# An SSM scan with a gated FFN behind it: when the last matmul part of a side piece is issued

## The chip, the cores and the metric

The kernel runs on one core of one Trainium2 chip. The metric is the device time of one execution in microseconds (us). The kernel before takes 2835.29 us, the median of three runs (2834.98 to 2836.63).

## The reference, cut to what matters

The input `x` holds 2 sequences of 1024 tokens with 512 features (float32). The first layer is a selective state space model, the second a gated FFN; behind each stands a layernorm over the residual sum.

```python
# layer 0, SSM: B=2, L=1024, D=512, N=R=128
xn    = x * rsqrt(mean(x*x) + 1e-6) * norm_w
xn    = xn * sigmoid((xn @ select_proj_w.T + select_proj_b) * select_gate)
xp    = xn @ x_proj_w.T                     # delta | B | C, 128 columns each
delta = softplus(xp[..., :R] @ dt_proj_w.T + dt_proj_b)
A     = -exp(A_log)
def step(h, (dt, bt, ct, xt)):              # once per token, h is [B, D, N]
    h = exp(dt[:, :, None] * A) * h + (dt * xt)[:, :, None] * bt[:, None, :]
    y = einsum('bdn,bn->bd', h, ct)
x = layernorm(x + (y + x * D_param) @ out_proj_w.T)
# layer 0, FFN: 2048 hidden features
x = layernorm(x + (silu(x @ w_gate.T) * (x @ w_up.T)) @ w_down.T)
```

## The kernel before, in words

**Groups and slots.** The 2048 tokens are cut into 64 blocks of 32 (`S`). A block has 16 groups of work, so the main loop (L673) runs over 1024 groups `k`. A group brings one scan: 128 partitions (the state index n), 32 features and 32 tokens, 1024 elements in a row (L716). `place` (L398) turns `k` into a half block `h = k // 8` and a slot `r = k % 8`.

**What one group issues.** TensorE (PE) gets four matmuls that each use 32 of its rows: two that write `bu`, the input of this group's scan (L696), and two that write `a`, the exponents of the next group's decay (L408 in `decay_mm`). ScalarE (ACT) takes two exponentials of `a` into `a_sb` (L415, `decay_exp`). VectorE (DVE) adds the carried state to the first column of `bu` (L715) and runs the scan (L716) into `h`. GpSimd (POOL) spreads `dt` and `du` over a block diagonal for later groups (`diag`, L379 and L389). The matmuls of `y` (L432, `y_round`) follow in slots 1, 4 and 7, eight rounds for each half block (`ROUNDS`, L22). `bu` and the PSUM tile of `a` have two buffers each, `a_sb` has three.

**Side work.** All else is written as Python generators that the loop steps through: `pre` prepares the inputs of the next lot of tokens (lots of 128, 128 and then 256 tokens, L69), `post` takes `y` of 128 tokens to the first layernorm, `ffn` makes the FFN of 128 tokens, and `silu` and `normalize` are short helpers. A generator yields "P" where it wants to begin a piece of matmuls, "H" while the piece has matmuls left and "E" where work of other engines follows. A *piece* is what goes into one tile of the single PSUM bank that `misc` (L158) hands out in the loop; a *part* is what is issued between two yields. `gu` (gate and up projections, L539) has 8 parts of two matmuls, `d` (down projection, L559) 16 parts of one, `op` (output projection, L480) 8 of one, `sel`, `xp` and `ss` 4 of one, `zT`, `x1T` and `uT` 2 of two transposes, `z` 2 of one, `b` one or two of four, `t0` (L307) a single part of four.

**What sets the order.** The slots 0, 2, 3, 5 and 6 get credit for side parts: `PARTS` (L23) is (4, 0, 3, 3, 0, 3, 3, 0), 16 parts for eight groups. Credit that isn't used is kept up to 6, and one group takes at most four parts (L725 to L729). `Work.tensor` (L636) takes the next part of the piece that holds the bank; when the piece is at its end the function returns False until the bank is read out, which `give_back` (L622, at the start of a slot with credit) or `others` (L629, once per group behind the exponentials) does. So a group can end one piece or begin one, but cannot do both.

**What must be ready when.** `load` (L333) fetches the operands of the next block out of DRAM at slot 0 of every second half block. Where the next block belongs to a new lot, `work.finish` (L689) first steps the side work until that lot's `pre` is done. The last steps of `pre` write two or three results, `uT` once or twice (L291) and `t0` (L314), through one and the same SBUF tile (tag "row", a single buffer) and from there to DRAM (L296, L315).

**Queues.** Every DMA is issued by SyncE (SP) in program order: weights of the FFN (L513, five buffers), `ub` and `cd` (L337, L345), `ub_d` (L259, L296), `x1`, `zT`, outputs.

**The end.** Behind the loop stand the last eight `y` rounds, and then the side work that is left, with six PSUM banks and no credit (L753).

Of the kernel before, what the change touches and what calls it, by code (L numbers as in the profile page):

```python
# [35 lines left out]
def kernel(  # L36
# [118 lines left out]

    made = {}

    def misc(name):  # L158
        return bank_pool[0].tile([P, 512], FP, tag="m", name=name)


# [3 lines left out]
    def pre(c):  # L165

        t0, n = lots[c]
        n_j, n_s = n // P, n // S
        if c == 0:
            xT = first_xT  # L170
        else:
            xT = pre_pool.tile([P, NM, TC], FP, tag="xT", name=f"xT_{c}")
            nc.sync.dma_start(xT[:, :, 0:n], x_tr[:, :, t0 : t0 + n])
        rms = pre_pool.tile([P, TC], FP, tag="rms", name=f"rms_{c}")
        low = pre_pool.tile([P, TC], FP, tag="low", name=f"low_{c}")
        dt = pre_pool.tile([P, NM, TC], FP, tag="dt", name=f"dt_{c}", bufs=2)
        u = pre_pool.tile([P, NM, TC], FP, tag="u", name=f"u_{c}")
        c_sb = pre_pool.tile([P, TC], FP, tag="c_sb", name=f"c_sb_{c}", bufs=2)
        rms, low, c_sb = rms[:, 0:n], low[:, 0:n], c_sb[:, 0:n]
        xT, dt, u = xT[:, :, 0:n], dt[:, :, 0:n], u[:, :, 0:n]  # L180
        xn = xT
        made[c] = dt, c_sb

        def matmuls(ps, w, m, rhs):
            for k in range(NM):
                nc.tensor.matmul(  # L186
                    ps[:, 0:n], w[:, k, ts(m, P)], rhs[:, k, :],
                    start=(k == 0), stop=(k == NM - 1),
                )
                yield "H" if k + 1 < NM else "E"  # L190

        yield "E"
        yield "E"
        yield "E"

        nc.scalar.activation(u, xT, AF.Square)
        yield "E"
        for m in range(NM):
            nc.scalar.activation(xT[:, m, :], xT[:, m, :], AF.Copy, scale=col(V_NORM, m))
        yield "P"  # L200
        ps = misc(f"ss_{c}")
        for k in range(NM):
            nc.tensor.matmul(  # L203
                ps[:, 0:n], ones, u[:, k, :], start=(k == 0), stop=(k == NM - 1)
            )
            yield "H" if k + 1 < NM else "E"

        nc.scalar.activation(rms, ps[:, 0:n], AF.Ln, bias=eps_r, scale=1.0 / D)
        nc.scalar.activation(rms, rms, AF.Exp, scale=-0.5)
        yield "E"  # L210
        for a in (slice(0, 2), slice(2, 4)):
            nc.gpsimd.tensor_tensor(
                xn[:, a, :], xT[:, a, :], rms.unsqueeze(1).to_broadcast([P, 2, n]), ALU.mult
            )
            yield "E"
        yield "P"


        for m in range(NM):
            ps = misc(f"sel_{c}_{m}")  # L220
            yield from matmuls(ps, sel_w, m, xn)
            nc.scalar.activation(
                u[:, m, :], ps[:, 0:n], AF.Relu,
                bias=neg[:, 1, m : m + 1], scale=neg[:, 0, m : m + 1],
            )
            nc.scalar.activation(
                dt[:, m, :], ps[:, 0:n], AF.Abs, bias=gate_b[:, m : m + 1], scale=col(V_GATE, m)
            )
            yield "P" if m + 1 < NM else "E"
        yield from softplus(dt, u)  # L230
        nc.scalar.activation(dt, dt, AF.Exp, scale=-1.0)
        yield "E"
        for a in (slice(0, 2), slice(2, 4)):
            nc.gpsimd.tensor_tensor(xn[:, a, :], xn[:, a, :], dt[:, a, :], ALU.mult)
            yield "E"
        yield "P"

        if c == 0:
            decay()

        for g, dst in ((0, low), (2, c_sb)):
            ps = misc(f"xp_{c}_{g}")
            yield from matmuls(ps, xp_w, g, xn)
            nc.scalar.copy(dst, ps[:, 0:n])
            yield "P"

        ps = misc(f"b_{c}")
        for j in range(n_j):
            for k in range(NM):
                nc.tensor.matmul(  # L250
                    ps[:, ts(j, N)], xn[:, k, ts(j, P)], xp_w[:, k, R : R + N],
                    start=(k == 0), stop=(k == NM - 1),
                )
            yield "H" if j + 1 < n_j else "E"
        bt = pre_pool.tile([P, TC // P, N], FP, tag="bt", name=f"bt_{c}")[:, 0:n_j, :]
        nc.scalar.copy(bt, ps[:, 0:n].rearrange("p (j n) -> p j n", n=N))
        for st in range(n_s):
            rows = bt[ts(st % 4, S), st // 4, :]
            nc.sync.dma_start(  # L259
                ub_d[t0 // S + st, :, :, 1, :].rearrange("g t n -> t g n"),  # L260
                rows.unsqueeze(1).to_broadcast([S, 4, N]),
            )
        yield "P"

        for a in range(0, NM, 2):
            ps = misc(f"z_{c}_{a}")
            for m in (a, a + 1):
                nc.tensor.matmul(  # L268
                    ps[:, ts(m - a, n)], dt_w[:, ts(m, P)], low, start=True, stop=True
                )  # L270
                yield "H" if m == a else "E"
            for m in (a, a + 1):
                z = ps[:, ts(m - a, n)]
                nc.scalar.activation(u[:, m, :], z, AF.Relu, bias=col(V_DTB, m))
                nc.scalar.activation(dt[:, m, :], z, AF.Abs, bias=col(V_DTB, m))  # L275
            yield "P" if a == 0 else "E"
        yield from softplus(dt, u)
        for a in (slice(0, 2), slice(2, 4)):
            nc.gpsimd.tensor_tensor(u[:, a, :], dt[:, a, :], xn[:, a, :], ALU.mult)
            yield "E"  # L280

        for j in range(n_j):
            yield "P"
            ps = misc(f"uT_{c}_{j}")
            for m in range(NM):
                nc.tensor.transpose(ps[:, ts(m, P)], u[:, m, ts(j, P)], ident)
                if m == 1:
                    yield "H"
            yield "E"
            t = pre_pool.tile([P, D], FP, tag="row", name=f"uT_{c}_{j}")  # L290
            nc.scalar.copy(  # L291
                t.rearrange("p (g m c) -> p m g c", g=4, m=NM),
                ps.rearrange("p (m g c) -> p m g c", m=NM, g=4),
            )
            for st in range(4):
                nc.sync.dma_start(  # L296
                    ub_d[t0 // S + 4 * j + st, :, :, 0, :].rearrange("g t q -> t g q"),
                    t[ts(st, S), :].rearrange("t (g q) -> t g q", g=4),
                )
            if c == 0:  # L300
                load(0)
                diag(0, 0)
                diag(0, 1)
        yield "P"
        ps = misc(f"t0_{c}")
        for m in range(NM):
            nc.tensor.matmul(  # L307
                ps[0:n_s, ts(m, P)],
                dt[:, m, :].rearrange("p (s t) -> p s t", t=S)[:, :, 0], ident,
                start=True, stop=True,  # L310
            )
        yield "E"
        t = pre_pool.tile([P, D], FP, tag="row", name=f"t0_{c}")
        nc.scalar.copy(t[0:n_s, :], ps[0:n_s, :])  # L314
        nc.sync.dma_start(dt0_d[t0 // S : (t0 + n) // S, :], t[0:n_s, :])  # L315
# [139 lines left out]
    def post(tt):  # L455
# [5 lines left out]
        nc.gpsimd.tensor_tensor(zT, zT, dq.unsqueeze(2).to_broadcast([P, NM, P]), ALU.mult)  # L461
        yield "E"
        yield "P"
        ps = misc(f"zT_{tt}")
        for s in range(4):
            nc.tensor.transpose(ps[:, ts(s, P)], yrs[tt][:, s, :], ident)
            if s == 1:
# [6 lines left out]
        x1 = post_pool.tile([P, D], FP, tag="x1", name=f"x1_{tt}", bufs=4)  # L474
        nc.sync.dma_start(x1, xf[tt])
        yield "P"
        ps = misc(f"op_{tt}")
        for half in (slice(0, 256), slice(256, 512)):
            for k in range(NM):
                nc.tensor.matmul(  # L480
# [19 lines left out]
    def ffn(tt, row):  # L500
# [17 lines left out]
        fetch(4)  # L518
        x1T = ffn_pool.tile([P, NM, P], FP, tag="x1T", name=f"x1T_{tt}")
        yield "P"  # L520
        ps = misc(f"x1T_{tt}")
        for m in range(NM):
            nc.tensor.transpose(ps[:, ts(m, P)], row[:, ts(m, P)], ident)
            if m == 1:
# [6 lines left out]
        for f in range(0, NF, 2):  # L531
            fetch(at + 4)
            yield "P"
            ps = misc(f"gu_{tt}_{f}")
            for b in range(2):
                w = pieces[at + b].rearrange("p (a k h) -> p a k h", a=2, k=NM)
                for a in range(2):
# [13 lines left out]
        for half in range(2):  # L551
            fetch(at + 4)
            yield "P"
            ps = misc(f"d_{tt}_{half}")
            for f in range(NF):
                if f == NH:
                    fetch(at + 6)
# [47 lines left out]
    class Work:  # L605


        def __init__(self):
            self.gens, self.holder = [], None

        def add(self, gen, front=False):
            item = [gen, next(gen)]
# [23 lines left out]
        def tensor(self):  # L636

            if self.holder is not None:
                if self.holder[1] != "H":
                    return False  # L640
                self.step(self.holder)
                return True
            for item in self.gens:
                if item[1] == "P":
                    self.holder = item
                    self.step(item)
                    return True
            return False

# [23 lines left out]
    for k in range(NG):  # L673
# [49 lines left out]
            for b in ROUNDS[r]:  # L723
                y_round(h - 1, b)
        credit = min(credit + PARTS[r], 6)  # L725
        for _ in range(min(credit, 4) if PARTS[r] else 0):
            if not work.tensor():
                break
            credit -= 1  # L729

        j, r4 = divmod(k, 4)
        if r4 == 3:
# [93 lines left out]
```

## Time and profile before

| what | value |
|---|---|
| median of 3 runs | 2835.29 us |
| the profiled execution: its time, and the span from its first to its last instruction | 2828.25 us, 2826.4 us |
| first scan, last scan (start, from the span's start) | 43.2 us, 2745.2 us |
| scans (L716) | 1024, mean 2286 ns |
| PE busy, DVE busy | 2711.6 us, 2518.8 us |
| `gu` matmuls (L539), `d` matmuls (L559) | busy 535.4 us, 256.9 us |
| DMA | 258.80 MB, 28% of the 16 engines' time |
| mean granted TensorE clock | 0.990 |

The table is read in two stages. Up to 2745 us the loop issues one scan after the other, and the distance from one scan's start to the next is the length of a step. Behind it come some 80 us without scans, in which PE works off what side work is left. A matmul in float32 shows as two records.

### The profile page before, as it was taken

Reading aid. Unit: us, or ns where it says so; the run is one execution under the profiler, and the core shown is the slowest. Engines: PE = TensorE matmul, PEld = TensorE weight load, DVE = VectorE, ACT = ScalarE, POOL = GpSimd, SP = SyncE. Lnnn points to the kernel's source line nnn. Section 1 sums busy time; section 2 is a strip of 40 time slices with the busy share of each in tenths; the row PEclk is TensorE's granted clock in tenths of the full one; section 3 lists DMA queues with packets and bytes.
Section 4 is the critical chain, followed back from the end, with each engine's and each line's share of the span. In section 5 each row is a group of like instructions: output and inputs, shape, how many; then the busy total and the mean of one; then the engine's idle time right before and its main releaser. Section 6 shows DMA issues by size and latency. Waiting matters only on the chain.

```text
span 2826.4 us, 59495 instructions
## 1 busy us (share of the span) xinstructions
PE 2711.6 (96%) x23744; PEld 1491.2 (53%) x23744; DVE 2518.8 (89%) x2144; ACT 1549.2 (55%) x3105; POOL 1780.9 (63%) x2016
## 2 busy tenths in 40 slices
PE   6879999999999999999999999999999999999998
PEld 4334554555555554555544555555555555555558
DVE  3999899999999999999999999999999999999980
ACT  4546555645565455654656556555555555545442
POOL 5556665666666665775667667667576666657552
PEclk7999999999999999999999999999999999999999
DMA  2002322324213232233312333133331323333336
GB/s 75 19 28 66 88 86 70 95 67 142 79 63 124 79 122 64 83 96 103 126 43 84 106 105 104 57 99 95 113 102 48 112 81 116 102 106 96 105 105 209
DMA packets 112388, 258.80 MB, mean 92 GB/s; under 512 B 11568, under 2 KB 49456, under 8 KB 112112
## 3 DMA queue, kind: packets, MB, share of 16 engines
q1 hardware_dynamic: 112112, 254.99, 28.2%
q8 instruction: 189, 3.10, 0.5%
q14 instruction: 87, 0.71, 0.1%
HBM read 242.23 MB, written 12.71 MB: 90 GB/s over the span
## 4 chain that ended last, share of the span: by engine, by line
PE 74%; DVE 18%; issue 3%; ACT 3%; POOL 1%; DMA 1%; SPq 0%; DVEq 0%; ACTq 0%; POOLq 0%
PE bu L696 28%; PE gu L539 17%; DVE h L716 16%; PE y L432 13%; PE d L559 7%; PE a L408 3%; PE sel L186 2%; PE op L480 2%; PE xp L186 1%; ACT a_sb L415 1%; DVE bu L715 1%; DMA ub_d<-uT 1%; PE b L250 1%; PE ss L203 0%; PE z L268 0%
## 5 line engine op out<-in xcount | busy, mean ns | idle before, releaser
L716 DVE TENSOR_TENSOR_SCAN h<-a_sb,bu 128x1024 f32<-128x1024 f32 x1024 | 2340.3, 2286 | 153.5 <-PE bu L696 44.6
L415 ACT ACTIVATE a_sb<-a 128x496 f32<-128x496 f32 x2048 | 1088.9, 584 | 1125.1 <-PE a L408 1049.6
L696 PE MATMUL bu<-du,ub 32*128 32x512 f32 x4096 | 1195.0, 644 | 49.4 <-DVE h L716 25.4
L408 PE MATMUL a<-ddt,a_t 32*128 32x512 f32 x4096 | 1224.1, 645 | 2.8 <-ACT t L314 2.8
L379 POOL TENSOR_TENSOR ddt<-dt,hot 128x512 f32<-128x512 f32 x512 | 533.6, 1048 | 218.6 <-PE a L408 218.6
L539 PEld LDWEIGHTS gu<-x1T,w 128*128 128x128 f32 x4096 | 479.7, 192 | 233.7 <-issue 153.6
L389 POOL TENSOR_TENSOR du<-ub,hot 128x512 f32<-128x512 f32 x512 | 535.3, 1049 | 26.7 <-PE a L408 23.3
L539 PE MATMUL gu<-x1T,w 128*128 128x128 f32 x4096 | 535.4, 282 | 11.7 <-ACT t L314 5.5
L432 PE MATMUL y<-h,cz 128*32 128x256 f32 x9208 | 526.8, 362 | 1.6 <-DVE h L716 1.0
L696 PEld LDWEIGHTS bu<-du,ub 32*128 32x128 f32 x4096 | 335.7, 184 | 345.0 <-issue 185.2
L432 PEld LDWEIGHTS y<-h,cz 128*32 128x32 f32 x9208 | 256.3, 110 | 408.9 <-issue 274.9
L408 PEld LDWEIGHTS a<-ddt,a_t 32*128 32x128 f32 x4096 | 354.7, 184 | 22.9 <-ACT a_sb L415 13.2
L559 PE MATMUL d<-w,hid 128*128 128x256 f32 x1024 | 256.9, 393 | 1.1 <-ACT dt L275 1.1
L715 DVE TENSOR_TENSOR bu<-bu,cd 128x32 f32<-128x32 f32 x992 | 183.3, 185 | 79.8 <-PE a L408 75.7
L559 PEld LDWEIGHTS d<-w,hid 128*128 128x128 f32 x1024 | 183.5, 189 | 121.6 <-issue 92.5
L577 POOL TENSOR_SCALAR gu<-gu 128x256 f32<-128x256 f32 x128 | 108.1, 844 | 198.7 <-ACT gu L547 198.0
L585 POOL TENSOR_TENSOR hid<-gu,e 128x256 f32<-128x256 f32 x128 | 92.8, 725 | 140.1 <-ACT e L583 139.2
L447 POOL TENSOR_TENSOR yc<-yc,pick 128x512 f32<-128x512 f32 x64 | 66.6, 1040 | 179.5 <-ACT yc L446 179.5
L366 POOL TENSOR_TENSOR cd<-cd,h 128x256 f32<-128x256 f32 x124 | 106.2, 857 | 43.9 <-DVE h L716 43.9
L578 POOL TENSOR_TENSOR gu<-gu 128x256 f32<-128x256 f32 x128 | 93.3, 729 | 10.7
L547 ACT COPY gu<-gu 128x512 f32<-128x512 f32 x128 | 75.2, 588 | 32.6 <-PE gu L539 32.2
L324 POOL TENSOR_TENSOR dt<-dt,u 128x512 f32<-128x512 f32 (+1 forms) x36 | 41.2, 1148 | 67.6 <-ACT dt L321 67.6
(86 smaller groups left out, 1246.0 us busy)
## 6 DMA issues: line engine op xcount, KB each, us to landing
w<-in_wgu_s_dram SPq DMA_DIRECT2D x256, 512.0 KB, 4.1
w<-in_wd_s_dram SPq DMA_DIRECT2D x128, 512.0 KB, 3.6
cd<-dt_d SPq DMA_DIRECT2D x62, 256.0 KB, 4.1
ub<-ub_d SPq DMA_DIRECT2D x64, 128.0 KB, 2.0
ub_d<-bt SPq DMA_DIRECT2D x64, 64.0 KB, 1.8
ub_d<-uT SPq DMA_DIRECT2D x64, 64.0 KB, 1.8
zT<-in_x_q_dram SPq DMA_DIRECT2D x16, 256.0 KB, 3.9
x<-in_x_dram SPq DMA_DIRECT2D x16, 256.0 KB, 3.7
```

The lines of the kernel that those rows point to most:

```text
L366: nc.gpsimd.tensor_tensor(cd, cd, last, ALU.mult)
L379: nc.gpsimd.tensor_tensor(ddts[j][:, m, :, :], made[lot_of[st]][0][:, a + m, toks(st)].unsqueeze(1).to_broadcast([P, 16, S]), hot[:, ts(i, ...
L389: nc.gpsimd.tensor_tensor(dus[j][:, m, :, :], uv[:, a + m, :].unsqueeze(2).to_broadcast([P, 16, S]), hot.unsqueeze(1).to_broadcast([P, 16, ...
L408: nc.tensor.matmul(ps, a_t[ts(g, 32), m, :], ddts[k // 4][ts(g, 32), m % 2, :, :], start=True, stop=True,)
L415: nc.scalar.activation(a_sb[:, k % 3, ts(b, 16), 1:], ps[:, :, 1:], AF.Exp, scale=-1.0)
L432: nc.tensor.matmul(ys[st][ts(m, 32), 256 * i + 4 * q0 : 256 * i + 4 * (q0 + nq)], cz[st % 3][:, at : at + 32], hs[h][:, 64 * m + q0 : 64 * ...
L539: nc.tensor.matmul(ps[:, ts(2 * a + b, P)], w[:, a, k, :], x1T[:, k, :], start=(k == 0), stop=(k == NM - 1),)
L559: nc.tensor.matmul(ps[:, 0:HD], hid[:, f, :], w[:, f % 4, :], start=(f == 0), stop=(f == NF - 1),)
L577: nc.gpsimd.tensor_scalar_max(g, g, -80.0)
L696: nc.tensor.matmul(bu[:, ts(b, 16), :], prepared[st][ts(g, 32), 1, :], dus[k // 4][ts(g, 32), m % 2, :, :], start=True, stop=True,)
L715: nc.vector.tensor_tensor(first, first, left[:, at : at + 2, i, :], ALU.add)
L716: nc.vector.tensor_tensor_scan(hs[h][:, ts(r, 32), :].rearrange("p q t -> p (q t)"), a_sb[:, k % 3, :, :].rearrange("p q t -> p (q t)"), b ...
```

## The change

`misc` now takes the number of parts of the piece that it opens and stores it in `work.left`; `Work.tensor` counts it down. The loop that hands out parts goes on while fewer than `most = min(credit, 4)` are taken, as before, and now also while at least one and fewer than five are taken and just one part of the piece is left. What is taken is subtracted from the credit, which can so become negative. A slot without credit of its own (1, 4, 7) still takes nothing.

```diff
--- before.py
+++ after.py
@@ -155,7 +155,8 @@
 
     made = {}
 
-    def misc(name):
+    def misc(name, parts):
+        work.left = parts
         return bank_pool[0].tile([P, 512], FP, tag="m", name=name)
 
 
@@ -198,7 +199,7 @@
         for m in range(NM):
             nc.scalar.activation(xT[:, m, :], xT[:, m, :], AF.Copy, scale=col(V_NORM, m))
         yield "P"
-        ps = misc(f"ss_{c}")
+        ps = misc(f"ss_{c}", NM)
         for k in range(NM):
             nc.tensor.matmul(
                 ps[:, 0:n], ones, u[:, k, :], start=(k == 0), stop=(k == NM - 1)
@@ -217,7 +218,7 @@
 
 
         for m in range(NM):
-            ps = misc(f"sel_{c}_{m}")
+            ps = misc(f"sel_{c}_{m}", NM)
             yield from matmuls(ps, sel_w, m, xn)
             nc.scalar.activation(
                 u[:, m, :], ps[:, 0:n], AF.Relu,
@@ -239,12 +240,12 @@
             decay()
 
         for g, dst in ((0, low), (2, c_sb)):
-            ps = misc(f"xp_{c}_{g}")
+            ps = misc(f"xp_{c}_{g}", NM)
             yield from matmuls(ps, xp_w, g, xn)
             nc.scalar.copy(dst, ps[:, 0:n])
             yield "P"
 
-        ps = misc(f"b_{c}")
+        ps = misc(f"b_{c}", n_j)
         for j in range(n_j):
             for k in range(NM):
                 nc.tensor.matmul(
@@ -263,7 +264,7 @@
         yield "P"
 
         for a in range(0, NM, 2):
-            ps = misc(f"z_{c}_{a}")
+            ps = misc(f"z_{c}_{a}", 2)
             for m in (a, a + 1):
                 nc.tensor.matmul(
                     ps[:, ts(m - a, n)], dt_w[:, ts(m, P)], low, start=True, stop=True
@@ -281,7 +282,7 @@
 
         for j in range(n_j):
             yield "P"
-            ps = misc(f"uT_{c}_{j}")
+            ps = misc(f"uT_{c}_{j}", 2)
             for m in range(NM):
                 nc.tensor.transpose(ps[:, ts(m, P)], u[:, m, ts(j, P)], ident)
                 if m == 1:
@@ -302,7 +303,7 @@
                 diag(0, 0)
                 diag(0, 1)
         yield "P"
-        ps = misc(f"t0_{c}")
+        ps = misc(f"t0_{c}", 1)
         for m in range(NM):
             nc.tensor.matmul(
                 ps[0:n_s, ts(m, P)],
@@ -461,7 +462,7 @@
         nc.gpsimd.tensor_tensor(zT, zT, dq.unsqueeze(2).to_broadcast([P, NM, P]), ALU.mult)
         yield "E"
         yield "P"
-        ps = misc(f"zT_{tt}")
+        ps = misc(f"zT_{tt}", 2)
         for s in range(4):
             nc.tensor.transpose(ps[:, ts(s, P)], yrs[tt][:, s, :], ident)
             if s == 1:
@@ -474,7 +475,7 @@
         x1 = post_pool.tile([P, D], FP, tag="x1", name=f"x1_{tt}", bufs=4)
         nc.sync.dma_start(x1, xf[tt])
         yield "P"
-        ps = misc(f"op_{tt}")
+        ps = misc(f"op_{tt}", 2 * NM)
         for half in (slice(0, 256), slice(256, 512)):
             for k in range(NM):
                 nc.tensor.matmul(
@@ -518,7 +519,7 @@
         fetch(4)
         x1T = ffn_pool.tile([P, NM, P], FP, tag="x1T", name=f"x1T_{tt}")
         yield "P"
-        ps = misc(f"x1T_{tt}")
+        ps = misc(f"x1T_{tt}", 2)
         for m in range(NM):
             nc.tensor.transpose(ps[:, ts(m, P)], row[:, ts(m, P)], ident)
             if m == 1:
@@ -531,7 +532,7 @@
         for f in range(0, NF, 2):
             fetch(at + 4)
             yield "P"
-            ps = misc(f"gu_{tt}_{f}")
+            ps = misc(f"gu_{tt}_{f}", 2 * NM)
             for b in range(2):
                 w = pieces[at + b].rearrange("p (a k h) -> p a k h", a=2, k=NM)
                 for a in range(2):
@@ -551,7 +552,7 @@
         for half in range(2):
             fetch(at + 4)
             yield "P"
-            ps = misc(f"d_{tt}_{half}")
+            ps = misc(f"d_{tt}_{half}", NF)
             for f in range(NF):
                 if f == NH:
                     fetch(at + 6)
@@ -606,7 +607,8 @@
 
 
         def __init__(self):
-            self.gens, self.holder = [], None
+
+            self.gens, self.holder, self.left = [], None, 0
 
         def add(self, gen, front=False):
             item = [gen, next(gen)]
@@ -638,12 +640,14 @@
             if self.holder is not None:
                 if self.holder[1] != "H":
                     return False
+                self.left -= 1
                 self.step(self.holder)
                 return True
             for item in self.gens:
                 if item[1] == "P":
                     self.holder = item
                     self.step(item)
+                    self.left -= 1
                     return True
             return False
 
@@ -723,10 +727,11 @@
             for b in ROUNDS[r]:
                 y_round(h - 1, b)
         credit = min(credit + PARTS[r], 6)
-        for _ in range(min(credit, 4) if PARTS[r] else 0):
-            if not work.tensor():
-                break
-            credit -= 1
+        done, most = 0, min(credit, 4)
+
+        while PARTS[r] and (done < most or 0 < done < 5 and work.left == 1) and work.tensor():
+            done += 1
+        credit -= done
 
         j, r4 = divmod(k, 4)
         if r4 == 3:
```

## The prediction, made before the changed kernel ran

> **What bounds the kernel now.** I read the page's busy shares and chain first, then the start of every scan in the timeline, then the largest steps, then the end.
>
> ```profile
> PE 2711.6 (96%) x23744; PEld 1491.2 (53%) x23744; DVE 2518.8 (89%) x2144; ACT 1549.2 (55%) x3105; POOL 1780.9 (63%) x2016
> PE 74%; DVE 18%; issue 3%; ACT 3%; POOL 1%; DMA 1%; SPq 0%; DVEq 0%; ACTq 0%; POOLq 0%
> L716 DVE TENSOR_TENSOR_SCAN h<-a_sb,bu 128x1024 f32<-128x1024 f32 x1024 | 2340.3, 2286 | 153.5 <-PE bu L696 44.6
> ```
>
> PE looks like the only bound. The 1023 steps between scan starts say something else: they add up to 2702.0 us, and more than half of them last 2.48 us, which is the scan and the add on DVE back to back. 1023 x 2.483 is 2540; the 162 us above sit in some 350 steps over 2.6 us. So DVE sets most steps, and PE sets those where more work came than PE can do in one step. Here are three groups with four `gu` parts each (slots 0, 2 and 3, about 998 to 1009 us), with a `y` group between the first two:
>
> ```profile
> 998.31 2.05 PE L539 MATMUL gu<-x1T,w 128*128 128x128 f32 x16
> ...
> 1003.86 2.05 PE L539 MATMUL gu<-x1T,w 128*128 128x128 f32 x16
> 1006.92 2.05 PE L539 MATMUL gu<-x1T,w 128*128 128x128 f32 x16
> ```
> ```profile
> 1002.25 2.29 DVE L716 TENSOR_TENSOR_SCAN h<-a_sb,bu 128x1024 f32<-128x1024 f32 x1
> 1004.45 0.17 DVE L715 TENSOR_TENSOR bu<-bu,cd 128x32 f32<-128x32 f32 x1
> 1004.73 2.29 DVE L716 TENSOR_TENSOR_SCAN h<-a_sb,bu 128x1024 f32<-128x1024 f32 x1
> ...
> 1010.14 0.20 DVE L715 TENSOR_TENSOR bu<-bu,cd 128x32 f32<-128x32 f32 x1 [0.47 <-PE a L408]
> 1010.44 2.29 DVE L716 TENSOR_TENSOR_SCAN h<-a_sb,bu 128x1024 f32<-128x1024 f32 x1
> ```
>
> Full groups follow on PE at 3.05 us (1003.86 to 1006.92). The first step shown is still 2.48 us, as PE had run ahead; by the third full group the lead is gone and DVE waits 0.47 us. An average of PE can't tell this: what counts is how full groups are bunched.
>
> The largest step of all, 326.90 to 336.97 us, is no bunch:
>
> ```profile
> 326.90 2.29 DVE L716 TENSOR_TENSOR_SCAN h<-a_sb,bu 128x1024 f32<-128x1024 f32 x1
> 336.66 0.20 DVE L715 TENSOR_TENSOR bu<-bu,cd 128x32 f32<-128x32 f32 x1 [7.48 <-PE a L408]
> ```
> ```profile
> 328.75 0.58 ACT L291 COPY uT<-uT 128x512 f32<-128x512 f32 x1 [1.20 <-DMA ub_d<-uT]
> 332.68 0.57 ACT L314 COPY t<-t 8x512 f32<-8x512 f32 x1 [3.33 <-DMA ub_d<-uT]
> ```
>
> Before group 112 `work.finish` forces the rest of `pre` for the third lot. In the order of PE's instructions its two `uT` stand at groups 109 and 110 and `t0` directly ahead of group 112: three copies through the one "row" buffer, each waiting for the DMAs of the one before, and the matmuls of group 112 queued behind.
>
> **The change part by part.** I counted, in the PE order of both programs, the parts that each slot with credit takes in groups 0 to 1022. Beside them is the mean step that follows such a group, from the scan starts of before: no part 41 to 43 groups (2.480 us); one 57 to 9 (2.553); two 95 to 154 (2.619); three 141 to 145 (2.554); four 306 to 284 (2.824); five 0 to 5 (no row). The total rises only from 1896 to 1913 parts, since credit limits it: a last part taken early is paid back by the next group, which gets two instead of four.
>
> *The end of the loop.* Of the 17 parts, 16 are one half of a `d` piece that leaves the end; the last part of a `gu` piece goes too, but that lay under a wait for POOL. The end of before:
>
> ```profile
> 2747.55 3.64 PE L432 MATMUL y<-h,cz 128*32 128x256 f32 x58 [1.05 <-DVE h L716]
> ...
> 2755.88 5.41 PE L480 MATMUL op<-out_w,zT 128*128 128x256 f32 x16 [1.39 <-DVE zT L471]
> 2761.12 13.98 PE L559 MATMUL d<-w,hid 128*128 128x256 f32 x64
> 2774.93 0.60 PE L523 MATMUL x1T<-ident,x 128*128 128x128 f32 x4
> 2777.59 28.85 PE L539 MATMUL gu<-x1T,w 128*128 128x128 f32 x256 [2.05 <-ACT x1T L527]
> ```
>
> From the end of `y` (2751.2) to the first `gu` (2777.6) are 26.4 us. A `d` matmul is 13.98/32 = 0.437, a part of `gu` 2 x 28.85/128 = 0.451. The changed order puts the one remaining `d` half right behind `y`, then `zT`, `op`, `x1T`. So: `d` 7.0 (it now covers the read-out of `y`), `zT` 0.6, the wait for DVE 1.4, `op` 3.5 at 0.437 each or 5.4 as here, then what `d` used to cover, the normalizing of `x1` (end of `op` 2761.3 to the end of ACT's L496 at 2764.7: 3.4), then `x1T` to `gu` 2.7. That is 18.6 to 20.5, a gain of 5.9 to 7.8. I take 7.0.
>
> *The forced stop.* The changed order has `uT` of that lot at groups 104 and 106 and `t0` at 107, five groups ahead of the due one; nothing is forced. The step of 10.07 becomes an ordinary `y` step (mean 2.544): 7.5 gained. Both `uT` and `t0` still pass the one buffer. The six later lots do that unforced; only two lost time near it, 2.3 us (step behind group 310) and 1.5 (behind 440), so the price to expect is 3.8/6 = 0.6. I take 6.9 gained, bounds 5.2 (a loss of 2.3 here too) and 7.5.
>
> *The other steps.* By the counts above, without the forced step: 2 x 2.480 - 48 x 2.553 + 59 x 2.619 + 4 x 2.554 - 22 x 2.824 + 5 x (2.824 to 3.275, a four-part step and one part more) = -0.9 to +1.4. But a two-part step can't by itself cost more than one with three parts; its row carries the bunches ahead of it. So I count bunches: steps by how many of the last three slots with credit took at least four parts (groups 32 to 1021, excess over 2.483 in before): none 0.071, one 0.111, two 0.222, three 0.239. These go from 147, 397, 297 and 148 steps to 217, 322, 344 and 106: 70 x 0.071 - 75 x 0.111 + 47 x 0.222 - 42 x 0.239 = -2.9. I take this, as it follows what the timeline shows. Bounds: if PE set every step, 17 x 0.44 = 7.4 more, and 5 x 0.45 for the five-part groups: +9.7. If PE ran dry in each of the 48 one-part groups and that hole is now filled, -48 x 0.45 + 7.4 = -14.2.
>
> DMAs and copies are the same in number. SP's weight loads move with their pieces by a few groups; SP waits for PE to free `w` buffers 858 us in all, so its queue follows PE and isn't ahead of it. I cost this at nothing; the cover is that a piece begins with its weights fetched a piece ahead.
>
> Sum: -7.0 - 6.9 - 2.9 = -16.8 us. The profiled span of 2826.4 becomes 2809.6. That execution took 2828.25, 7.0 below the median of the runs, so I carry the difference over: 2835.3 - 16.8 = 2818.5.
>
> *The clock.* Behind the forced stop the granted clock is 0.50 for 3.4 us:
>
> ```profile
> 333.40:336.80 3.40, 3.40 (x13) 1.67 (x14) 0.14 (x1) 0.25 (x1) 0.00 (x0) 0.50 0.32 89
> ```
>
> The Trainium skill ("TensorE: Matmul & The Clock Gate", section "What's actually happening") says that PE falls to half its clock after an idle window of about 3.4 us and needs a busy one to come back. The trace agrees at this place. By that rule the newly exposed 3.4 us between `op` and `x1T` would start `gu` at half rate and take 3.4/2 = 1.7 back: a sum of -15.1, 2820.2 us. I leave it out of the sum, since the phase of the window isn't known.
>
> **The rivals.** *PE sets every step.* Then the 17 parts cost 7.4 in the loop, and only the stop and the end are left: -7.0 - 6.9 + 7.4 = -6.5, 2828.8 us. For it: 96% busy, 74% of the chain. Against it: the 2.48 us of most steps. [...]
>
> *Holes.* PE runs dry in the one-part groups and all of it comes back: -7.0 - 6.9 - 14.2 = -28.1, 2807.2. For: such a step is 2.55, though its PE work is little. Against: four-part groups that follow a one-part group already cost less (2.67 against 2.85 elsewhere), so part of the hole is used.
>
> *The stop only moves.* The row buffer stalls groups 104 to 107 for as long as it did before 112: -7.0 - 2.9 = -9.9, 2825.4.
>
> *ACT's queue (slower).* A piece ended one group sooner is read out sooner, by a copy that `give_back` puts ahead of the next exponentials; a `gu` copy takes 0.59 us (75.2/128). If all 48 one-part groups pay this in full, +28.3 - 16.8 = +11.5, 2846.8. It decides once ACT has under 0.59 us free ahead of the exponentials. Against it: ACT waits there for PE 1049.6 us in 837 waits, 1.25 each, and the scan waited for `a_sb` once, 0.5 us.
>
> **How the numbers follow.** Chances: the forecast 0.62 (its own range 2811 to 2825), holes 0.13, PE everywhere 0.13, the stop moves 0.05, ACT's queue 0.07. A measurement of this kernel can tell 0.2%, 5.7 us. Faster takes the first, holes, the moved stop and 0.08 of the second rival: 0.88. Within 0.2% takes the remaining 0.05; slower is 0.07. The range 2808 to 2829 leaves out ACT's queue and the far half of holes and of PE everywhere, some 0.2.
>
> **What would show it.** The end from the last `y` to the first `gu` of about 19 to 20 us, with one `d` half in it. No step near 10 us; steps at groups 104 to 108 under 5. About 30 fewer steps over 2.6 us, their loss gone where four, four, four became four, two, four. Wrong: if steps behind two-part groups rise, PE sets them (second rival); if waits of the scan for `a_sb` appear, ACT does; if SP's weight loads land behind the matmuls that need them, the term that I set to nothing.

## The result and the profile after

The changed kernel takes 2806.97 us, the median of 4 runs (2805.25 to 2809.71), beside 2835.96 for the kernel before. The ratio is 0.989 with a 95% interval of 0.9874 to 0.9906. Six further executions (below) gave 0.9901 (0.9883 to 0.9918); all ten together have a median of 2808.8. The forecast was 2818.5 with a range of 2808 to 2829: the right direction, and 11.5 us too little of the gain (9.7 by all ten).

The page of the changed kernel; busy shares, the chain by engine, and two groups (busy, mean ns, idle before). Lines are shifted by up to four against the kernel before (L716 is now L720, L715 L719, L408 L409).

```profile
PE 2688.0 (96%) x23744; PEld 1476.3 (53%) x23744; DVE 2514.2 (90%) x2144; ACT 1549.9 (55%) x3105; POOL 1782.9 (64%) x2016
...
PE 74%; DVE 17%; issue 3%; ACT 3%; POOL 2%; DMA 1%; SPq 0%; DVEq 0%; POOLq 0%; ACTq 0%
...
L720 DVE TENSOR_TENSOR_SCAN h<-a_sb,bu 128x1024 f32<-128x1024 f32 x1024 | 2340.5, 2287 | 154.8 <-PE bu L700 43.5
...
L719 DVE TENSOR_TENSOR bu<-bu,cd 128x32 f32<-128x32 f32 x992 | 182.5, 184 | 65.5 <-PE a L409 61.5
```

The shares are those of before within one percent, on a span that is 22.9 us shorter (2803.5 against 2826.4). What moved is the wait: DVE's add waited 75.7 us for the matmuls of `a` in before (167 times) and now 61.5. By stage, from the scan starts of both profiles: the first scan 43.2 to 42.1 us, the loop 2702.0 to 2686.1, the end behind the last scan 81.2 to 75.3. In the loop, groups 64 to 127 give 9.0 us and all later ones 7.0 (6.6 of it up to group 511); the first 64 give none. Behind group 512 the changed kernel does 15 parts more in the same time.

**Four, two, four.** The same slots as in the block shown of before, PE first (groups 360, 362 and 363 with four, two and four parts), then DVE:

```profile
985.47 2.05 PE L540 MATMUL gu<-x1T,w 128*128 128x128 f32 x16
...
988.53 1.50 PE L433 MATMUL y<-h,cz 128*32 128x256 f32 x24
...
991.03 1.16 PE L540 MATMUL gu<-x1T,w 128*128 128x128 f32 x8
...
993.33 2.05 PE L540 MATMUL gu<-x1T,w 128*128 128x128 f32 x16
```
```profile
991.81 2.29 DVE L720 TENSOR_TENSOR_SCAN h<-a_sb,bu 128x1024 f32<-128x1024 f32 x1
994.02 0.18 DVE L719 TENSOR_TENSOR bu<-bu,cd 128x32 f32<-128x32 f32 x1
994.30 2.29 DVE L720 TENSOR_TENSOR_SCAN h<-a_sb,bu 128x1024 f32<-128x1024 f32 x1
996.55 0.20 DVE L719 TENSOR_TENSOR bu<-bu,cd 128x32 f32<-128x32 f32 x1
```

The two-part group takes 2.30 us on PE (991.03 to 993.33) instead of 3.05, less than a step, so PE gets its lead back before the next full group. The add at 996.55 has no wait, where before it stood 0.47 us.

Where nothing but `gu` is at hand, the slots 0, 2, 3, 5 and 6 took four, four, four, three and one part before, and take four, two, four, four and two now, 16 both times. The second order isn't free of waits: in groups 368 to 375 the steps take 1.3 us more than 8 x 2.483 before and 1.0 after, as slot 5 now pays 0.39. Over all half blocks from group 128 on that do exactly 16 parts, this excess is 1.26 us on average before (67 half blocks) and 1.02 after (73); the second profiles of both kernels (below) give 1.29 and 1.02. Most of that lies in groups 128 to 511 (1.46 to 1.01; behind 512 it is 1.11 to 1.04), and the ten or so half blocks with 18 parts got dearer (1.66 to 2.13).

**No forced stop.** ACT's copies of the third lot, and DVE in the same stretch:

```profile
310.00 0.60 ACT L292 COPY uT<-uT 128x512 f32<-128x512 f32 x1
...
314.04 0.59 ACT L292 COPY uT<-uT 128x512 f32<-128x512 f32 x1 [1.45 <-DMA ub_d<-uT]
...
317.83 0.57 ACT L315 COPY t<-t 8x512 f32<-8x512 f32 x1
```
```profile
308.54 2.29 DVE L720 TENSOR_TENSOR_SCAN h<-a_sb,bu 128x1024 f32<-128x1024 f32 x1
311.58 0.20 DVE L719 TENSOR_TENSOR bu<-bu,cd 128x32 f32<-128x32 f32 x1 [0.75 <-PE a L409]
311.88 2.29 DVE L720 TENSOR_TENSOR_SCAN h<-a_sb,bu 128x1024 f32<-128x1024 f32 x1
```

One copy still waits 1.45 us for the DMA of the one before, but the longest step near it is 3.34 us, and none is near 10.

**The end.** PE behind the loop, and one window of it (busy time and count of PE, PEld, DVE, ACT, POOL, then the granted clock, DMA share, GB/s):

```profile
2730.53 3.64 PE L433 MATMUL y<-h,cz 128*32 128x256 f32 x58 [1.05 <-DVE h L720]
2734.11 7.17 PE L560 MATMUL d<-w,hid 128*128 128x256 f32 x32
2741.12 0.60 PE L467 MATMUL zT<-ident,yr 128*128 128x128 f32 x4
2743.32 3.72 PE L481 MATMUL op<-out_w,zT 128*128 128x256 f32 x16 [1.61 <-DVE zT L472]
2750.55 0.96 PE L524 MATMUL x1T<-ident,x 128*128 128x128 f32 x4 [3.50 <-ACT x L497]
2752.18 31.40 PE L540 MATMUL gu<-x1T,w 128*128 128x128 f32 x256 [0.68 <-ACT x1T L528]
```
```profile
2750.70:2757.50 6.80, 6.12 (x29) 5.72 (x29) 0.00 (x0) 0.59 (x1) 0.00 (x0) 0.50 0.46 167
```

From the end of `y` (2734.2) to the first `gu` (2752.2) are 18.0 us instead of 26.4, 8.4 less. Then `gu` takes 31.40 us instead of 28.85: the 3.50 us in which PE waited for the normalizing were followed by 6.8 us at half clock. Net 5.9. All four profiles of kernels with this end show the 6.8 us and a `gu` of 31.1 to 31.5.

### The profile page after: what moved, and what is told of

Read it like the earlier page. It is cut to its first block, busy times and chain, and to the rows that moved or that the text cites. A ratio compares the mean times of both kernels' runs of the same rounds, so it can differ in the third digit from the quotient of the medians.

```text
span 2803.5 us, 59499 instructions
## 1 busy us (share of the span) xinstructions
PE 2688.0 (96%) x23744; PEld 1476.3 (53%) x23744; DVE 2514.2 (90%) x2144; ACT 1549.9 (55%) x3105; POOL 1782.9 (64%) x2016
## 4 chain that ended last, share of the span: by engine, by line
PE 74%; DVE 17%; issue 3%; ACT 3%; POOL 2%; DMA 1%; SPq 0%; DVEq 0%; POOLq 0%; ACTq 0%
PE bu L700 28%; PE gu L540 17%; DVE h L720 15%; PE y L433 12%; PE d L560 8%; PE a L409 3%; ACT a_sb L416 1%; PE sel L187 1%; PE op L481 1%; PE xp L187 1%; DVE bu L719 1%; DMA ub_d<-uT 1%; PE b L251 1%; PE ss L204 1%; SPq L297 0%
## 5 line engine op out<-in xcount | busy, mean ns | idle before, releaser
L720 DVE TENSOR_TENSOR_SCAN h<-a_sb,bu 128x1024 f32<-128x1024 f32 x1024 | 2340.5, 2287 | 154.8 <-PE bu L700 43.5
L409 PE MATMUL a<-ddt,a_t 32*128 32x512 f32 x4096 | 1209.0, 643 | 2.8 <-ACT t L315 2.8
L390 POOL TENSOR_TENSOR du<-ub,hot 128x512 f32<-128x512 f32 x512 | 535.9, 1051 | 21.8 <-PE a L409 18.5
L700 PEld LDWEIGHTS bu<-du,ub 32*128 32x128 f32 x4096 | 329.2, 184 | 352.4 <-issue 190.2
L409 PEld LDWEIGHTS a<-ddt,a_t 32*128 32x128 f32 x4096 | 347.9, 184 | 15.9 <-ACT a_sb L416 9.2
L719 DVE TENSOR_TENSOR bu<-bu,cd 128x32 f32<-128x32 f32 x992 | 182.5, 184 | 65.5 <-PE a L409 61.5
```

The lines of the kernel that those rows point to most:

```text
L390: nc.gpsimd.tensor_tensor(dus[j][:, m, :, :], uv[:, a + m, :].unsqueeze(2).to_broadcast([P, 16, S]), hot.unsqueeze(1).to_broadcast([P, 16, ...
L409: nc.tensor.matmul(ps, a_t[ts(g, 32), m, :], ddts[k // 4][ts(g, 32), m % 2, :, :], start=True, stop=True,)
L700: nc.tensor.matmul(bu[:, ts(b, 16), :], prepared[st][ts(g, 32), 1, :], dus[k // 4][ts(g, 32), m % 2, :, :], start=True, stop=True,)
L719: nc.vector.tensor_tensor(first, first, left[:, at : at + 2, i, :], ALU.add)
L720: nc.vector.tensor_tensor_scan(hs[h][:, ts(r, 32), :].rearrange("p q t -> p (q t)"), a_sb[:, k % 3, :, :].rearrange("p q t -> p (q t)"), b ...
```

## The experiments

Each was timed beside the kernel before on the same chip. Over all of them that kernel ran 56 times besides its two profiles, 2829.9 to 2848.2 us with a median of 2837.3. "Excess" is what the steps of a stretch take over 2.483 us each.

**1 and 2. The rule early, the rule late.** `0 < done < 5 and work.left == 1` gets one more condition:

```diff
-        while PARTS[r] and (done < most or 0 < done < 5 and work.left == 1) and work.tensor():
+        while PARTS[r] and (done < most or k < 112 and 0 < done < 5 and work.left == 1) and work.tensor():
```

(and `k >= 112` in the second).

> The changed rule in groups 0 to 111 alone; from group 112 on the old rule. 1895 parts in the loop (before: 1896), so the end keeps its two d halves; uT of the third lot at groups 104 and 106, t0 at 107. If the forced stop before group 112 costs what its step shows, the loop gets 7.6 us shorter there plus 1 to 2 us of smaller steps around it, and the end stays: 8 to 10 us less in all. If the stop only moves with the three copies through the row buffer, a step of 5 us or more appears at groups 104 to 108 and the gain is under 4 us. If what the whole change gained over the forecast (29 us at the medians against 16.8) comes from the early part, this gains 15 us or more.

> The changed rule from group 112 on alone; the forced stop stays. 1919 parts in the loop (23 more than before), 42 d matmuls at the end instead of 64. Bunching theory: the end gets 6 to 9 us shorter, the loop 4 to 8 us shorter in spite of 23 parts more, 10 to 17 us in all, and the step of 10 us at group 111 is still there. PE sets every step: the loop gets 23 x 0.44 = 10 us longer, the end 6 to 9 us shorter, so 1 to 4 us slower in all.

Early: 2817.18 us (2816.57 to 2818.05) beside 2837.51, ratio 0.9929 (0.9902 to 0.9955). Groups 64 to 127 fall from 18.5 to 10.8 us of excess and the end stays (81.6), so the stop is worth what its step showed; no step of 5 us takes its place. But 20 us at the medians are twice what was expected, and by the medians the third case (15 or more) would hold, while the profile against the first profile of before gives 10.1. That gap pointed at the first profile itself. The early rule also moves later work: 12 parts fewer stand in groups 128 to 511, where the excess falls from 67.4 to 56.8, and 11 more behind group 512, where it rises from 75.7 to 81.3.

Late: 2822.68 us (2816.88 to 2828.7), ratio 0.9953 (0.9936 to 0.997), 15 us faster with 23 parts more in the loop and the stop still there (step of 9.9 us). "PE sets every step" wanted it 1 to 4 us slower and falls by the medians. The loop of its profile doesn't settle it: 2706.3 us, 4.3 more than in the first profile of before and 9.4 less than in the second, where 4 to 8 less was expected. The two gains don't add up to that of the whole (35 against 29).

**3. More parts, no regrouping.**

```diff
-        credit = min(credit + PARTS[r], 6)
+        credit = min(credit + PARTS[r] + (1 if r == 0 and 560 <= k < 836 else 0), 6)
```

> The old rule, with one more credit at slot 0 of groups 560 to 835: 13 parts more in the loop, 12 d matmuls fewer at the end, no regrouping (54 one-part groups, 308 full ones). If PE sets the steps, the loop gets 13 x 0.44 = 5.7 us longer and the end 5 to 6 us shorter: no change within 1.5 us. If the loop has slack for parts, the loop stays within 2 us and the total gains 4 to 6 us; then the shorter end of the changed kernel is a true gain whatever the grouping. If more parts add to bunches, the loop loses 6 us or more.

2836.65 us beside 2837.51, ratio 1.0 (0.9984 to 1.0016): no change. The end is 74.3 us instead of 81.2, and behind group 512 the loop's excess rises from 75.7 to 83.0, 0.56 us for each of the 13 parts. DVE's waits for the matmuls of `a`, before first, then this kernel (us, times, longest):

```profile
DVE bu L715 <- PE a L408: 75.7, 167, 7.5
```
```profile
DVE bu L715 <- PE a L408: 88.2, 174, 7.7
```

A part moved from the end into the loop is no gain as such.

**4. Two row buffers in the kernel before.**

```diff
-            t = pre_pool.tile([P, D], FP, tag="row", name=f"uT_{c}_{j}")
+            t = pre_pool.tile([P, D], FP, tag="row", bufs=2, name=f"uT_{c}_{j}")
...
-        t = pre_pool.tile([P, D], FP, tag="row", name=f"t0_{c}")
+        t = pre_pool.tile([P, D], FP, tag="row", bufs=2, name=f"t0_{c}")
```

> The old rule, the row tile of uT and t0 with two buffers instead of one; the order of the matmuls is that of before. If the wait of the copies for the DMAs of the one buffer makes the forced stop long, the step behind group 111 falls from 10.1 us to 5 or 6 us, the steps behind groups 310 and 440 lose their 2.3 and 1.5 us, and the total falls by 5 to 9 us. If the stop is made of the forced matmuls and the DMA round trip of the operands, it stays at 9 to 10 us and the total doesn't move by 2 us.

2824.31 us (2815.55 to 2824.78), ratio 0.9944 (0.9922 to 0.9967). DVE at the forced stop, which in before was 326.90 to 336.97:

```profile
332.62 2.29 DVE L716 TENSOR_TENSOR_SCAN h<-a_sb,bu 128x1024 f32<-128x1024 f32 x1
337.46 0.20 DVE L715 TENSOR_TENSOR bu<-bu,cd 128x32 f32<-128x32 f32 x1 [2.56 <-POOL cd L366]
337.76 2.29 DVE L716 TENSOR_TENSOR_SCAN h<-a_sb,bu 128x1024 f32<-128x1024 f32 x1
```

The step falls from 10.07 to 5.14 us and those behind groups 310 and 440 lose their excess: the single buffer made 4.9 us of the stop, as expected, and what is left waits for POOL's product for the carried state (`cd`, 2.56 us). The total moved by 13 us at the medians, more than the 5 to 9 expected and again beyond what the steps show.

**5. Regrouping without more parts.** The changed rule and one credit less at slot 0 of groups 620 to 835: 1895 parts in the loop, as in before, 9 one-part groups (before 57) and 275 with four parts or more (before 306, changed kernel 289).

```diff
-        credit = min(credit + PARTS[r], 6)
+        credit = min(credit + PARTS[r] - (1 if r == 0 and 620 <= k < 836 else 0), 6)
```

> The changed rule with one credit less at slot 0 of groups 620 to 835, so that the loop takes 1895 parts, as before the change (1896); the end has its two d halves again. This is the regrouping without the 17 parts more. As priced in the prediction (stop 6.9 to 7.6, bunches 2.9 for all else, parts free) the loop is 10 us shorter than before. If each part in the loop costs its 0.44 us there, as the run with 13 parts more showed (loop 13 us longer at one profile, 7 of them behind group 512, end 7 us shorter), the changed kernel's loop of 16 us less hides 7.4 us paid for parts, and this loop is 22 to 24 us shorter than before, with an end as long as before: 2807 us, like the changed kernel. If the parts were free in the loop, the total is 2813.

2803.49 us (2802.78 to 2806.39), ratio 0.9874 (0.9857 to 0.989). The loop is 2678.2 us, 23.8 less than in the first profile of before, as the second case said, and 37.5 less than in the second profile; the end is 84.1. DVE's waits for the matmuls of `a` in this kernel:

```profile
DVE bu L719 <- PE a L409: 57.2, 137, 2.6
```

So regrouping, the end of the stop included and without a part more in the loop, is worth the whole gain. Against the changed kernel's first profile the excess behind group 512 falls from 75.3 to 63.3 for 18 parts fewer, 0.67 each, while a part at the end costs 0.44 to 0.45. But this edit also leaves 14 full groups fewer, so 0.67 isn't the price of the number alone; the 0.56 of experiment 3, which hardly regroups (308 full groups, 54 with one part), is nearer to that. Both are loop times of single profiles. That the 17 parts cost more in the loop than they save is seen at the medians only (2803.5 against 2808.8, partly on other chips): the first profiles of the two kernels are level, 2804.6 and 2803.5 us of span.

**6 and 8. The rule with two row buffers, and with the credit edit too** (the edits of 4, then of 4 and 5, in the changed kernel).

> The changed rule and two row buffers together. If the two cures are for the same stop, the sum is not additive: the change has already removed the stop, and only the waits of the later lots (steps behind groups 259, 310 and 440: 2.4, 2.3 and 1.2 us in the changed kernel) are left to gain, 3 to 6 us, near 2802. If they are additive, 2807 - 13 = 2794.

> The changed rule, two row buffers and one credit less at slot 0 of groups 620 to 835 (1895 parts). If the end has room for parts at their bare price and bunches are what the loop pays for, this is 3 to 5 us faster than the same without the credit edit: near 2799. If parts cost the same in the loop and at the end, the same within 2 us.

2806.61 us (2801.94 to 2810.88) and 2803.94 (2802.99 to 2805.7). The two cures don't add up: both are for the one stop. The steps behind groups 310 and 440 fall to 2.48 us. The one behind 259 is at 3.25, but the second profile of the changed kernel has 3.26 there with one buffer too, and no copy through "row" stands near it (groups 184 to 187 and 306 to 309); that this step waits for the buffer was wrong. At the medians the second buffer gives 2 us, inside the spread, where 3 to 6 were expected; the credit edit on top gives 2.7, with ranges that overlap, so neither case of its expectation can be told (near 2799, or the same within 2 us).

Experiments 4 and 8 differ by the rule and the credit edit, that is by the regrouping alone: both have two buffers, 1896 and 1895 parts in the loop, and a dear start (7.2 and 9.9 us of excess in the first 64 groups). From group 64 on the excess falls from 152.1 to 128.5 us, 23.6 less, of which 2.7 is what was left of the stop; the medians differ by 20.4.

**7. The kernel before once more, for a second profile.**

> The kernel before once more, for a profile. 17 runs of it gave 2830 to 2845 us at mean granted clocks of 0.989 to 0.983, so their spread looks like a matter of the clock: 0.001 of mean clock is 2.8 us at full rate against none, and every window of 3.4 us at half clock lowers the mean by 0.0006 and should cost 1.7 us. If so this profile's time stands to that of the first (2828 us, 11 windows) as the number of windows does. If the spread comes from elsewhere (DMA), the number of windows doesn't tell the time.

2841.73 us. Of the 13.6 us by which its span exceeds the first one's, 9.6 lie in the first 64 groups. Two windows in which both profiles ran the start; the second kernel shown is the first profile of before (columns as above):

```profile
43.00:70.00 27.00, 27.00 (x85) 14.45 (x87) 20.58 (x9) 12.22 (x26) 13.83 (x15) 0.50 0.01 2
```
```profile
43.00:70.00 27.00, 25.13 (x138) 12.45 (x137) 24.25 (x11) 16.09 (x35) 15.19 (x17) 0.81 0.01 2
```

At a granted clock of 0.50 all through, PE issues 85 records where it issued 138, and DVE gets 9 instructions instead of 11. In all, the first profile spent 59.3 us at half clock and this one 86.9: at full rate against none that is worth 13.8 us, close to the 13.6. The first profile, 2828.25 us, lies below every other run. Over 37 runs of before a straight line gives 2.3 us for each 0.001 of mean granted clock (medians 2841.7 at 0.985, 2836.4 at 0.987, 2833.2 at 0.989); 2.8 was expected.

**9. The changed kernel once more.**

> The changed kernel once more, for the spread of its runs beside that of before. Two profiles of before (2826.4 and 2840.0 us of span) differ by 9.6 us in the first 64 groups and by 4 us in all else, so the first was a cheap draw. If the start is a draw for the changed kernel as well, its runs spread over some 10 us too (2805 to 2816) with a median near 2810, and the difference of the medians shrinks from 29 to some 26 us. If the change itself makes the start cheaper, its runs stay within 2804 to 2810 while those of before reach 2845.

2809.46 us: five runs from 2808.27 to 2810.42 and one of 2817.76 at a clock of 0.985. The first case holds in part: the runs spread over 10 us here too. But the profile has only 2.1 us of excess in the first 64 groups (0.3 in the first profile), and the difference of the medians didn't shrink: 29.6 us, ratio 0.9901 (0.9883 to 0.9918). At equal clocks, over the runs up to here, the gap is 26.2 us at 0.987 (2836.4 to 2810.2), 27.6 at 0.988 (2836.6 to 2809.0) and 24.8 at 0.989 (2833.2 to 2808.4).

**10 and 12. PE kept busy at the start.** In the changed kernel, and in the same manner in the kernel before (both do 192 matmuls beyond the reference's work):

```diff
         credit -= done
+        if PARTS[r] and done == 0 and k < 128 and work.holder is None:
+            warm = misc(f"warm_{k}", 0)
+            for _ in range(6):
+                nc.tensor.matmul(warm[:, 0:P], ones, ident, start=True, stop=True)
```

> The changed kernel with six matmuls of 128x128x128 that nobody reads (0.23 us each) in every slot with credit of groups 0 to 127 that takes no part while the bank is free: 192 of them, beyond the reference's work. If the half-clock windows of the start come from PE's idle time there, the windows between the spans 60 and 230 us go, the first 64 groups cost under 2 us above 2.483 each in sum, and the spread shrinks to under 4 us, at a median of 2801 to 2806. If they come from elsewhere, or if full groups at half clock aren't what makes the start long, the 192 matmuls change nothing or cost up to 5 us.

> The kernel before with the same 192 unread matmuls in the first 128 groups as the filled changed kernel (2809.7 us, runs within 4 us). If the draw of the start is what spreads the runs of before (2828 to 2848) and widens the gap of the medians, this kernel's runs stay within 5 us near 2828 to 2831, the first 64 groups cost under 3 us above the floor, and the gap between the filled kernels is 19 to 22 us: the change without the draw. If the spread has another cause, the median stays near 2838 and the gap near 28 us.

The changed kernel filled takes 2809.7 us (2807.54 to 2811.15), the one before filled 2834.14 (2829.69 to 2841.73). The clock did what was expected. Filled changed kernel first, the changed kernel's first profile below:

```profile
121.00:200.00 79.00, 77.60 (x748) 43.77 (x740) 75.77 (x63) 35.90 (x68) 45.30 (x50) 1.00 0.07 20
200.00:230.00 30.00, 30.00 (x283) 16.57 (x280) 28.13 (x25) 17.97 (x35) 16.92 (x19) 1.00 0.12 33
```
```profile
121.00:200.00 79.00, 59.15 (x556) 22.63 (x556) 75.25 (x64) 36.99 (x71) 44.24 (x48) 0.98 0.06 18
200.00:230.00 30.00, 25.29 (x220) 11.91 (x220) 28.76 (x25) 18.88 (x37) 19.08 (x20) 1.00 0.08 28
```

No half-clock window is left between 60 and 300 us in either filled profile. But DVE is as busy as before, 75.77 against 75.25 us: single windows between 120 and 230 us cost little, as PE has time to spare there, and the changed kernel gains nothing, where a median of 2801 to 2806 was expected in the first case. The filled kernel before has 1.0 us of excess in the first 64 groups, as expected, and is 2.4 us faster than the unfilled one beside it (2836.53). The gap between the filled kernels is 24.4 us, or 26.9 when each is taken against the kernel before on its own chip; 19 to 22 was expected. And the runs of the filled kernel before still spread over 12 us. So the start's draw is 2 to 5 us of the 29, and not all of the spread; what makes the rest of the spread isn't shown.

**11. All of it together:** the kernel of 8 with the fill of 10.

> The kernel with the changed rule, two row buffers and one credit less in late slots 0 (2804 us), and the same unread matmuls at the start. Its one profile has 9.9 us above the floor in the first 64 groups; if the fill takes that to 2 us, 2796 us. If the fill does nothing, 2804.

2795.9 us (2792.93 to 2798.48), ratio 0.9848 (0.983 to 0.9866), 13 us below the changed kernel. Excess in the first 64 groups is 0.8 us, against 9.9 in the profile of 8: there the long half-clock stretch at the start (39.6 to 70.3 us) was what the fill took away (in this kernel half clock ends at 45.5 us).

## Why the prediction was right or wrong

*Direction and places: right.* All three places that it named got shorter, and no stretch of 64 groups elsewhere got longer by more than 2.2 us. The signs came as described, some of them larger: 18.0 us from the last `y` to `gu` (19 to 20 forecast), no step near 10 us, 54 steps fewer over 2.6 us (348 to 294; some 30 forecast), and the steps behind two-part groups fell (2.619 to 2.562). The weight loads were rightly set to nothing: the longest wait of PE's loads for one is 0.8 us.

*The forced stop: right.* Priced at 6.9 us (bounds 5.2 to 7.5); the step gave 7.6, its 64 groups 9.0, and the early rule alone shows it without the rest. The rival "the stop only moves" falls with the steps of at most 3.34 us.

*The end: right in size, for a reason that was left out.* Forecast 7.0, measured 5.9. The stretch up to `gu` gave 8.4, above the bound of 7.8, and `gu` at half clock took 2.55 back. The half clock behind a wait of some 3.4 us was weighed from the Trainium skill ("TensorE: Matmul & The Clock Gate", section "What's actually happening") at 1.7 and left out of the sum. The trace agrees that half clock follows such a wait (here 3.50 us); it lasted two of those lengths, 6.8 us, so that 2.55 was lost and not 1.7.

*As a gain, the end was misread.* The prediction let the parts that leave the end cost next to nothing in the loop. Experiment 3 shows 0.56 us for each, experiment 5 at most 0.67, regrouping included.

*The other steps: the term that was mis-sized.* "I take this, as it follows what the timeline shows": -2.9. Measured, profile against profile: the loop's 16.0 less the stop's 7.6, so -8.4, and that with the price of 17 parts in it. From group 64 on, the two profiles of each kernel give -6.0 to -12.3 in their four pairings. Without the parts (experiment 5) it is 23.8 - 7.6 = 16.2 less, and between experiments 4 and 8 it is 23.6 - 2.7 = 20.9. The mechanism was the named one, four, two, four. What failed is the table of bunches: steps by how many of the last three slots took at least four parts, in any order, at the prices of before. The counts moved to exactly what was forecast (217, 322, 344 and 106 steps), but the row of two, priced at 0.222, mixed two kinds of steps. In before, 151 steps directly behind two full slots in succession cost 0.331 each, the other 146 of the row 0.109. After the change the first kind has 146 steps at 0.334 and the second 198 at 0.083. So the 47 steps that the row gained were all of the cheap kind. With that row split, the prices of before give -9.4 over groups 32 to 1021, where -10.1 was measured (-6.1 in the second profile of the changed kernel). The split was chosen after the result and isn't a full price list: for experiment 5 it gives -12.3 where -17.6 was measured, for experiment 3 -0.9 where it was 5 to 11 more.

*Bounds and luck.* For the regrouping by itself the lower bound, 48 one-part groups with a hole of 0.45 us each, 21.6, was nearer than -2.9: 16.2 is three quarters of it, 20.9 nearly all. With the parts in it, -8.4 lies halfway between the forecast's -2.9 and the -14.2 of "holes". That the total of "holes", 2807.2, fits the median is luck in part: its term is 5.8 too large, and the base made up 3.5 of that.

*The base: wrong.* "I carry the difference over": the profiled execution stood 7.0 below the median, and the prediction treated that as a constant. It was a draw, the fastest of all runs of that kernel and the one with the highest mean clock (0.990); the changed kernel's median of ten lies only 3.5 above its profiled run (2808.8 to 2805.3). So the 9.7 us between forecast and median are 3.5 of base and 6.2 of terms (5.5 the other steps, 1.1 an earlier first scan, 0.7 the stop, less 1.1 for the end). Profile against profile the gain is 22.9; at equal clocks, and between the filled kernels, 24 to 28. What is left up to 29 at the medians goes with the changed kernel's higher mean clock (median 0.988 against 0.987). Whether the change itself makes the start's draw cheaper stays open: no run has profiled enough starts.

*The rivals.* "PE sets every step" is right that a part costs its time in the loop (0.56 us in experiment 3, even above its 0.44), and its conclusion is wrong: experiment 5 gains 35 us at the medians with no part moved out of the end. "ACT's queue" didn't come: the scan waited for `a_sb` 2.7 us in all.

## What to carry to other kernels

Where two engines take turns at being the bound, count how work is bunched per step, not how much there is: as many parts as before cost 24 us less in the loop, profile against profile, once almost none stood alone; 16 of the 24 lie in ordinary steps. In a table of such steps keep the order: directly behind two full groups in succession a step cost three times what it cost behind as many that stood apart or further back (0.331 and 0.109 us). Moving work from an idle end into a full loop isn't a gain in itself; price it on both sides, by an edit that moves work alone. And before a forecast is made against one profile, ask which draw it is: its mean granted clock beside that of other runs costs nothing to look at.

## What the runs showed of the hardware that was not expected

The spread of one program's time goes with its mean granted clock, 2.3 us for each 0.001 over 37 runs. In the one pair of profiles 9.6 of 13.6 us arise in the first 64 groups, where PE has little side work to do. There the excess is 0.3 or 9.9 us for the same program, and it goes with how long the half clock lasts after the first scan: in the eight unfilled profiles in which that stretch ended at 53 to 56 us the first 64 groups cost 0.3 to 4.5 us, in the three in which it ran on to some 70 us they cost 7.2 to 9.9. A PE that the records show as busy doesn't bring the clock back by that alone: from 43 to 70 us it was busy for all of 27.00 us in the slow draw, at a granted clock of 0.50. By these records the rule that the prediction weighed, that a busy window brings the clock back, did not hold there; why stays open.

192 matmuls that nobody reads, 0.23 us each, took the half-clock windows away between 60 and 300 us. That made the best kernel 8 us faster (2803.9 to 2795.9), the kernel before 2.4 us, and the changed kernel not at all.
